# One projection of an attention layer by two levels of block products, with its operand sums formed on GpSimd

## The chip, the cores and the metric

The kernel runs on one core of a Trainium2 chip. The core's engines work side by side, each through its own queue in order: TensorE multiplies matrices and writes its sums to PSUM, VectorE and ScalarE move results out of PSUM and do elementwise work, GpSimd (POOL in the profile) does elementwise work on SBUF, and SyncE (SP) issues most of the DMA transfers between DRAM and SBUF. The metric is the device time of one execution in microseconds. Three runs of the kernel before took 1883.57 to 1885.51 us, with a median of 1883.69.

## The reference

Input x is 8 images of 512 channels and 32 x 32 = 1024 places, in float32. Four layers follow one another:

- Layer 0: a linear attention with 64 channels, scaled by the largest singular value, and a residual.
- Layer 1: group normalization, then attention over the 1024 places with 512 channels:

```python
h = _group_norm(x, gamma, beta).reshape(B, C, N)
q, k, v = wq h + bq, wk h + bk, wv h + bv
attn = softmax(q^T k * C ** -0.5)
out = x + wp (v attn^T) + bp
```

- Layer 2: attention with 128 channels, and a residual.
- Layer 3: signs of x times signs of a 512 x 512 matrix, scaled, and a leaky slope.

The kernel multiplies wq and wk once, into a 512 x 512 matrix wu. The scores of layer 1 are then h^T u with **u = wu h + bu**, a 512 x 512 by 512 x 1024 product for each of the 8 batches. This u is what the change is about.

## The kernel before

**Stages.** A setup computes statistics of layer 0 over all batches, wu and wo = wv wp, and their block sums. Then `fast` runs once for each batch, in the order 6, 7, 0, 1, ..., 5. It computes for one batch: the scores of layer 1 (`scores1`), v (`make_v`), the values and the residual (`values1`), the projections of layer 2 (`project2`), its scores (`scores2`), its values (`values2`), their projection back (`close2`, L683), and layer 3 (`leave`). Work of the next batch is woven in by generators that are stepped at fixed places: `entering` (the end of layer 0 and the normalization), `make_u` for its u, and the previous batch's last half of layer 3 (`rest3`).

**Block products.** `seven` multiplies two matrices, each cut into 2 x 2 blocks, with seven block products in place of eight. It needs sums of blocks: `sums_of` makes S1 to S4 of the left factor, `differences_of` makes T1 to T4 of the right one, on VectorE. The seven products are, in order, A11 B11, S1 T1, S2 T2, S4 B22, S3 T3, A12 B21, A22 T4. Each is accumulated in PSUM by `product_of` (matmuls at L396). `seven` moves results out on ScalarE (L348, L350) and adds them on VectorE (L354, L356). For u the left blocks are 256 x 256 blocks of wu (kept with su, their sums, in SBUF), the right ones 256 x 512 blocks of h (h and hs). `make_u` does it in two passes of 128 output rows each: 2 x 7 block products of 2 matmuls on 512 columns, 28 matmuls for a batch. It has 14 steps. At the last, `sums_of` forms S1 to S4 of u itself (tile us), because u is the left factor of the next batch's scores. S1 is the sum of the two quarters u's second column half consists of (below: c12, upper channels, and c22, lower channels); c21, the lower quarter of the first half, is needed only for S4.

**Where the steps of u stand.** `fast` steps `make_u` once at each of the last three steps of `project2`, once after every second tile of `scores2` (four times), once ahead of the values, once after them, twice inside `leave`, and the rest after `close2` of the second half. So steps 1 to 8 lie among the projections and scores of layer 2, and steps 9 to 14 at the batch's end, right before the next batch's `scores1`, which needs the whole u.

**What sets the order.** In the main part a scheduler orders each engine's queue, by priority in the order of the program text and by its own idea of when inputs are ready; waits on semaphores are put in by it. At run time every queue is in order. PSUM has eight banks of 128 x 512; an access to one half of a bank is ordered after earlier accesses to the other half.

**GpSimd before.** It has 109 instructions: the setup's constants, small powers (L236, L1085, L1182), and the residual sums of `values1` (L578, L604) and, in the last batch, of `leave` (L743).

**SyncE before.** In the order of its queue for each batch: a store and two loads around the inverse row sums of each attention (`inverse_sums`, L847 to L855), the stores of the output (L761), the loads of the next x (L139) and of f (L292).

After all batches a branch (`verdict`) leads to a general version of the whole computation if a row sum is out of bounds.

Of the kernel before, what the change touches and what calls it, by code (L numbers as in the profile page):

```python
# [16 lines left out]
P = 128  # L17
B = 8
C = 512
N = 1024  # L20
CC = C // P
NT = N // P
HF = 512
# [62 lines left out]
def kernel(  # L86
# [17 lines left out]
    nc = tc.nc  # L104
    mm = nc.tensor.matmul
# [17 lines left out]
    def bank():  # L123
        return psum["bank"].tile([P, HF], F32, tag="bank", name="bank")
# [17 lines left out]
    def half(i):  # L142
        return bass.ts(i, HF)
# [100 lines left out]


    r_dram = [dram.tile([4, N // 4], F32, name=f"r_dram{i}") for i in range(2 * B)]
    f_dram = [dram.tile([P, HF], F32, name=f"f_dram{b}") for b in range(B)]
    gm = [keep.tile([P, P], F32, tag=f"gm{j}", name=f"gm{j}") for j in range(NPAIR)]
    gs_, gh_ = (
# [18 lines left out]

    wu = wpool.tile([P, CC, C], F32, tag="wu", name="wu")
# [5 lines left out]
    su = wpool.tile([P, 3, 2, C // 2], F32, tag="su", name="su")  # L277
    so = wpool.tile([P, 3, 2, C // 2], F32, tag="so", name="so")


# [195 lines left out]
    def split_h(env, ht):  # L476
        hs = env["big"].tile([P, 3, 2, HF], F32, tag="hs", name="hs")
        b = [ht[:, chunks[k], half(n)] for k in range(2) for n in range(2)]
        return differences_of(b, [hs[:, i] for i in range(3)])

    def make_u(env, hb, got):

        ut = env["big"].tile([P, CC, N], F32, tag="uv", name="ut")
        wa = weights["u"]

        def done():
            us = env["big"].tile([P, 3, 2, HF], F32, tag="us", name="us")
            got.append(
                sums_of(quarters_of(ut, chunks, [half(0), half(1)]), [us[:, i] for i in range(3)])
            )  # L490

        for i in range(2):
            term = product_of(
                lambda a, b, q, k: wa[a][:, k, bass.ts(i, P)],
                lambda a, b, q, k: hb[b][:, k, :],
            )
            yield from seven(
                term,
                ut[:, i, half(0)],
                ut[:, i, half(1)],  # L500
                ut[:, 2 + i, half(0)],
                ut[:, 2 + i, half(1)],
                bu[:, i : i + 1],
                bu[:, 2 + i : 3 + i],
                then=done if i else None,
            )

    def make_v(hb, vt):

# [383 lines left out]
    def fast(env, n, hb, ua):  # L893
# [43 lines left out]
        for k, _ in enumerate(values1(env, xt, vt, es, r, scratch)):  # L937
            chore(k in (2, 7, 9, 11, 13))
            if k == 5 and more:
                nxt = resident[order[n + 1]]  # L940
                hb = split_h(env, normal(env, nxt))
        signs = None
        if more:
            steps = make_u(env, hb, got)
        else:
            signs = unpacked(env)

# [642 lines left out]
    with ExitStack() as main:  # L1590
        psum_pools(main, 0, 8)
        big = main.enter_context(tc.tile_pool(name="big", bufs=1, reuse_waits="tile"))
        epool = main.enter_context(tc.tile_pool(name="epool", bufs=EBUFS))
        small = main.enter_context(tc.tile_pool(name="small", bufs=3))
        env.update({"big": big, "e": epool, "small": small})
        got = []
        hb = split_h(env, normal(env, resident[order[0]], True))

        for k, _ in enumerate(make_u(env, hb, got)):
            if k in (1, 4, 7, 10, 13):  # L1600
                next(behind)
        ua = got[0]
        for n in range(B):
            hb, ua = fast(env, n, hb, ua)

# [113 lines left out]
    with tc.If(verdict[0] > 0):  # L1719
        with (  # L1720
            ExitStack() as stack,
            tc.tile_pool(name="gbig", bufs=1) as big,
            tc.tile_pool(name="gepool", bufs=4) as epool,
            tc.tile_pool(name="gsmall", bufs=2) as small,
        ):
            env = {"big": big, "e": epool, "small": small}
            psum_pools(stack, 2, 4)

            for a in (weights["u"], weights["o"]):
                nc.vector.tensor_tensor(a["S3"], a["A11"], a["S3"], ALU.subtract)  # L1730
            for b in range(B):
                xt = load_x(b)
                general(env, xt, b, channels(out[b]))
# [42 lines left out]
```

## Time and profile before

| | |
|---|---|
| median of three runs | 1883.69 us |
| profiled execution, its own time | 1883.24 us |
| its span, from first to last instruction | 1881.5 us |
| TensorE busy | 1857.0 us |
| VectorE busy | 1118.1 us |
| ScalarE busy | 545.7 us |
| GpSimd busy | 121.8 us |
| DMA traffic | 66.51 MB |
| granted TensorE clock, mean | 0.997 |

The page's first part gives for each engine its busy time, its share of the span and its number of instructions. A group's line names the source line, the engine, the operation, output and inputs, the form and the count, then the busy time and the mean length of one in ns, and the idle time of the engine ahead of the group with what ended it. A line of the timeline gives start, length, engine, source line and count, and in brackets the idle time ahead of it and its releaser. Consecutive matmuls overlap in the records, so one's cost is read from the distance of starts. In the timeline, one batch's u goes from 566 us to 637 us.

### The profile page before, as it was taken

How to read it: one execution, taken by the hardware profiler on the slowest of the kernel's cores; microseconds unless marked ns; L12 is line 12 of the kernel's file. 1: busy time of each engine (PE TensorE's matmuls, PEld its weight loads, DVE VectorE, ACT ScalarE, POOL GpSimd, SP SyncE). 2: the span in 40 equal slices, each digit the busy share in tenths (PEclk: the TensorE clock that was granted, in tenths of full speed). 3: DMA queues.
4: the chain of work that ended last, by engine and by line, in shares of the span. 5: the costliest groups of instructions: out<-in, count | busy, mean ns of one | idle time of the engine just before them, and what ended most of it. 6: DMA issues, size and time to landing. Idle time of an engine off the chain costs nothing.

```text
span 1881.5 us, 16558 instructions
## 1 busy us (share of the span) xinstructions
PE 1857.0 (99%) x6244; PEld 952.1 (51%) x6244; DVE 1118.1 (59%) x2077; ACT 545.7 (29%) x888; POOL 121.8 (6%) x109
## 2 busy tenths in 40 slices
PE   8998999999999999999999999999999999999997
PEld 3365455544645455544645455544645464544653
DVE  3256776467764676567764676357643666355447
ACT  2142221144202521244202522144202521244113
POOL 1000001100020000100020001100020001000011
PEclk9999999999999999999999999999999999999999
DMA  8420000002000200002000200001000200000001
GB/s 324 161 79 7 1 18 1 1 34 73 12 1 12 84 23 1 1 34 73 12 1 11 78 30 0 1 34 67 12 0 12 90 12 0 1 34 23 12 0 47
DMA packets 25203, 66.51 MB, mean 35 GB/s; under 512 B 3553, under 2 KB 4765, under 8 KB 24477
## 3 DMA queue, kind: packets, MB, share of 16 engines
q1 hardware_dynamic: 24188, 64.96, 9.5%
q8 instruction: 51, 0.84, 0.2%
q10 hardware_dynamic: 864, 0.43, 0.1%
q14 instruction: 36, 0.29, 0.0%
q0 software_dynamic: 64, 0.00, 0.0%
HBM read 46.44 MB, written 18.94 MB: 35 GB/s over the span
## 4 chain that ended last, share of the span: by engine, by line
PE 96%; DVE 2%; ACT 1%; issue 0%; DMA 0%; POOL 0%; DVEq 0%; ACTq 0%
PE bank L396 46%; PE bank L565 21%; PE bank L967 6%; PE bank L814 6%; PE bank L1354 5%; PE bank L666 3%; PE bank L683 3%; PE bank L420 1%; PE bank L706 1%; PE wide L1394 1%; PE bank L1450 1%; PE bank L1035 1%; PE bank L837 0%; PE quad L1248 0%; PE bank L1141 0%
## 5 line engine op out<-in xcount | busy, mean ns | idle before, releaser
L565 PE MATMUL bank<-e,vt 128*128 128x512 f32 x768 | 336.2, 594 | 0.0
L565 PEld LDWEIGHTS bank<-e,vt 128*128 128x128 f32 x768 | 144.3, 190 | 172.3 <-issue 167.9
L396 PE MATMUL bank<-ut,h 128*128 128x512 f32 x384 | 178.3, 597 | 0.0
L396 PEld LDWEIGHTS bank<-ut,h 128*128 128x128 f32 x384 | 71.3, 190 | 95.2 <-issue 93.5
L814 PE MATMUL bank<-tpg 128*128 128x512 f32 x256 | 115.4, 595 | 0.0
L396 PE MATMUL bank<-us,hs 128*128 128x512 f32 x256 | 115.3, 592 | 0.0
L967 PE MATMUL bank<-e,tpg 128*128 128x512 f32 x256 | 114.7, 595 | 0.0
L354 DVE TENSOR_TENSOR e<-bank,e 128x512 f32<-128x512 f32 x96 | 66.1, 689 | 63.2 <-PE bank L396 44.7
L821 ACT ACTIVATE e<-bank 128x512 f32<-128x512 f32 x128 | 76.3, 597 | 67.0 <-PE bank L814 67.0
L396 PE MATMUL bank<-wo,h 128*128 128x256 f32 x384 | 89.9, 384 | 0.0
L348 ACT COPY e<-bank 128x512 f32<-128x512 f32 x96 | 56.1, 584 | 115.0 <-PE bank L396 114.6
L396 PE MATMUL bank<-h,wu 128*128 128x512 f32 x192 | 89.4, 595 | 0.0
L236 POOL TENSOR_TENSOR r_r<-r_v,minus_half 128x4 f32<-128x4 f32 (+1 forms) x11 | 10.9, 988 | 1073.4 <-DVE r_v L235 1067.9
L967 PEld LDWEIGHTS bank<-e,tpg 128*128 128x128 f32 x256 | 48.1, 190 | 60.4 <-issue 60.0
L396 PEld LDWEIGHTS bank<-us,hs 128*128 128x128 f32 x256 | 48.6, 190 | 58.4 <-issue 55.7
L396 PEld LDWEIGHTS bank<-wo,h 128*128 128x128 f32 x384 | 71.4, 190 | 12.6 <-issue 3.8
L826 DVE TENSOR_TENSOR esum<-esum,e 128x1024 f32<-128x1024 f32 x48 | 58.8, 1225 | 30.2 <-ACT e L821 30.0
L814 PEld LDWEIGHTS bank<-tpg 128*128 128x128 f32 x256 | 47.6, 190 | 55.0 <-issue 52.4
L694 ACT ACTIVATE sg<-xt,rb 128x512 f16<-128x512 f32 x64 | 44.2, 716 | 107.4 <-DVE xt L685 104.5
L354 DVE TENSOR_TENSOR vt<-bank,vt 128x512 f32<-128x512 f32 x48 | 33.2, 691 | 67.3 <-PE bank L396 66.6
L348 ACT COPY vt<-bank 128x512 f32<-128x512 f32 x64 | 37.3, 583 | 122.3 <-PE bank L396 122.3
L348 ACT COPY ut<-bank 128x512 f32<-128x512 f32 x48 | 28.1, 585 | 123.4 <-PE bank L396 123.4
(367 smaller groups left out, 2927.0 us busy)
## 6 DMA issues: line engine op xcount, KB each, us to landing
xt<-in_x SPq DMA_DIRECT2D x55, 512.0 KB
out<-both SPq DMA_DIRECT2D x63, 256.0 KB
rfull<-r_dram SPq DMA_DIRECT2D x15, 512.0 KB
f_dram<-f SPq DMA_DIRECT2D x8, 256.0 KB
fb<-f_dram SPq DMA_DIRECT2D x8, 256.0 KB
w<-in_w SPq DMA_DIRECT2D x1, 1024.0 KB
q<-in_w_q SPq DMA_DIRECT2D x1, 1024.0 KB
k<-in_w_k SPq DMA_DIRECT2D x1, 1024.0 KB
```

What stands on the lines that cost most here:

```text
L348: nc.scalar.copy(dst, ps)
L354: nc.vector.tensor_tensor(dst, ps, u, ALU.add)
L396: mm(out=ps[:, q * w : (q + 1) * w], lhsT=lt(ka, kb, q, k), rhs=rhs(ka, kb, q, k), start=first and q == 0 and k == 0, stop=last and k == 1 ...
L565: mm(out=ps, lhsT=a[:, t, bass.ts(r_, P)], rhs=e[t], start=first and t == 0, stop=last and t == NTH - 1, skip_group_check=True,)
L666: mm(out=ps[:, i, :], lhsT=xt[:, cc, bass.ts(4 * h + i, P)], rhs=sbw["tpg"][:, cc, 2 * P : 3 * P], start=cc == 0, stop=cc == CC - 1,)
L683: mm(out=ps, lhsT=sbw["z"][:, bass.ts(oc, P)], rhs=att, start=True, stop=True)
L694: nc.scalar.activation(sg[:, cc, :], xt[:, cc, half(h)], AF.Sign, bias=rb3[:, cc : cc + 1])
L814: mm(out=ps, lhsT=pt[:, 0, bass.ts(t, P)], rhs=tt[:, 0, half(h)], start=True, stop=True,)
L821: nc.scalar.activation(e[:, half(h)], ps, AF.Exp, scale=float(P) ** -0.5)
L826: nc.vector.tensor_tensor(esum, esum, e, ALU.add)
L967: mm(out=banks[h], lhsT=gt[:, t, :], rhs=es[t][:, half(h)], start=t == 0, stop=t == NT - 1,)
L1354: mm(out=banks[i][side(h), :], lhsT=w0[i][:, cc, :], rhs=xt[:, cc, half(h)], start=cc == 0, stop=cc == CC - 1,)
```

## The change

For the first batch of the order u is made as before. For the other seven, `make_u2` takes the place of `make_u`:

- **Two levels.** Each of the seven block products (256 x 256 by 256 x 512) is itself done by seven products of 128 x 128 by 128 x 256 blocks (`inner`): 49 matmuls on 256 columns for a batch. `inner` uses two banks, p1 and p2, each for two half-bank results, in two steps: four products (A11 B11, S2 T2 in p1; S1 T1, S3 T3 in p2), then three (A12 B21 onto the first; S4 B22 and A22 T4 onto p2's). Three ScalarE copies and five VectorE sums of 256 columns follow each `inner`. In what follows, product i (0 to 6) is the i-th of the outer seven in the order of `pairs`.
- **Factors from DRAM.** The seven 128 x 128 factors of each outer block are made once, in the first batch's `scores1` (`factors_of_u`: four GpSimd sums and three stores for each of the seven), and stored in `fac_dram`. Each product's factors (448 KB) are loaded from there in each batch, into one of two buffers.
- **Sums of h on GpSimd.** `prepare_u` forms the inner T1 to T4 of a product's right block with three GpSimd instructions (128 x 512, 128 x 256, 128 x 256), into one of two buffers. The first two products are prepared in `values1` ahead of u, product i + 2 after product i's second step.
- **Sums of u on GpSimd.** The outer products 0, 1, 3 and 4 are written straight into quarters of u, the others into temporary tiles; the outer sums are then made in place by GpSimd instructions of 128 x 1024 (four for a batch) and 128 x 512 (five), and one VectorE instruction for the second half of product 6. c12 gets two of the 1024-wide sums after product 4, c22 one after product 5.
- **Storage.** wu and su move to a pool (`first_u`) that is closed after the first u; the buffers for factors and sums take its place. wu is stored to DRAM in the setup and loaded again in the general version only.

The number of steps stays 14, and so do the places where they are stepped.

```diff
+    wu_dram = dram.tile([P, CC, C], F32, name="wu_dram")
+    fac_dram = [dram.tile([P, 7, P], F32, name=f"fac_dram{i}") for i in range(7)]
...
+    def factors_of_u(env):
+        tt = nc.gpsimd.tensor_tensor
+        for i, (a, _) in enumerate(pairs):
...
+            tt(s[:, 0], a21, a22, ALU.add)
+            tt(s[:, 1], s[:, 0], a11, ALU.subtract)
+            tt(s[:, 2], a11, a21, ALU.subtract)
+            tt(s[:, 3], a12, s[:, 1], ALU.subtract)
+            nc.sync.dma_start(out=fac_dram[i][:, 0:2], in_=w[:, :, 0:P])
+            nc.sync.dma_start(out=fac_dram[i][:, 2], in_=a22)
+            nc.sync.dma_start(out=fac_dram[i][:, 3:7], in_=s)
+            yield
+
+    def prepare_u(env, hb, i):
+        jit = env["jit"]
+        fac = jit.tile([P, 7, P], F32, tag="fac", name="fac", bufs=2)
+        nc.sync.dma_start(out=fac, in_=fac_dram[i])
+        b = hb[pairs[i][1]]
+        t = jit.tile([P, 4, QF], F32, tag="jit", name="jit", bufs=2)
+        lo, hi = slice(0, QF), slice(QF, HF)
+        tt = nc.gpsimd.tensor_tensor
+        tt(t[:, 0:2], b[:, :, hi], b[:, 0, :].rearrange("p (i n) -> p i n", i=2), ALU.subtract)
+        tt(t[:, 2], b[:, 1, hi], t[:, 0], ALU.subtract)
+        tt(t[:, 3], b[:, 1, lo], t[:, 2], ALU.subtract)
...
+    def inner(made, d, bias=None):
...
+        pa = product(p1[:, lo], 0, True, False)
+        nc.scalar.copy(d21, pa)
+        pb = product(p1[:, hi], 2, False, True)
+        nc.vector.tensor_tensor(d21, pb, d21, ALU.add)
+        pc = product(p2[:, lo], 3, True, False)
+        nc.scalar.copy(d12, pc)
+        pd = product(p2[:, hi], 5, False, False)
+        plus(d22, pd, d21, 1)
+        nc.vector.tensor_tensor(d22, d22, d12, ALU.add)
+        yield
+        product(pa, 1, False, True)
+        ...
+        product(pc, 4, False, True)
+        plus(d12, pc, d21, 0)
+        product(pd, 6, False, True)
+        plus(d21, pd, d21, 1)
+        yield
+
+    def make_u2(env, hb, got, made):
...
+        for i, (a, _) in enumerate(pairs):
+            direct = {0: (1, 0), 1: (0, 0), 3: (1, 1), 4: (0, 1)}.get(i)
...
+            for j, _ in enumerate(inner(made[i], d, bias)):
+                if j:
+                    if i == 1:
+                        add(c11, c21)
+                    elif i == 4:
+                        add(c12, c21)
+                        add(c12, c22)
+                    elif i in (2, 5, 6):
+                        for k in range(2):
+                            tt = (nc.vector if i == 6 and k else nc.gpsimd).tensor_tensor
+                            tt(c21[:, k, :], c21[:, k, :], d[k], ALU.add)
+                        if i == 5:
+                            add(c22, c21)
+                    if i + 2 < 7:
+                        made.append(prepare_u(env, hb, i + 2))
+                    if i == 6:
+                        us = env["big"].tile([P, 3, 2, HF], F32, tag="us", name="us")
+                        got.append(sums_of(...))
+                yield
...
+            if n == 0 and k in (9, 11, 13, 15, 17, 19, 21):
+                next(late_u)
...
                 hb = split_h(env, normal(env, nxt))
+                if "jit" not in env:
+                    first_u.close()
+                    env["jit"] = main.enter_context(
+                        tc.tile_pool(name="jit", bufs=1, side="right", reuse_waits="tile")
+                    )
+                made_u = [prepare_u(env, hb, i) for i in range(2)]
...
-            steps = make_u(env, hb, got)
+            steps = make_u2(env, hb, got, made_u)
...
+        nc.sync.dma_start(out=wu_dram, in_=wu)
```

More of the change, by code (lines that the diff above doesn't have):

```diff
@@ L267 @@
     bb2 = const.tile([P, CC], F32, tag="bb2", name="bb2")
-    wu = wpool.tile([P, CC, C], F32, tag="wu", name="wu")
+    first_u = ExitStack()
+    upool = first_u.enter_context(
+        tc.tile_pool(name="first_u", bufs=1, side="right", reuse_waits="tile")
+    )
+    wu = upool.tile([P, CC, C], F32, tag="wu", name="wu")
     wo = wpool.tile([P, CC, C], F32, tag="wo", name="wo")
@@ L275 @@
     bvo = const.tile([P, CC], F32, tag="bvo", name="bvo")
-    su = wpool.tile([P, 3, 2, C // 2], F32, tag="su", name="su")
+    su = upool.tile([P, 3, 2, C // 2], F32, tag="su", name="su")
     so = wpool.tile([P, 3, 2, C // 2], F32, tag="so", name="so")
@@ L506, in make_u @@
             )
+    pairs = [
+        ("A11", "B11"),
+        ("A12", "B21"),
+        ("S2", "T2"),
+        ("S1", "T1"),
+        ("S4", "B22"),
+        ("S3", "T3"),
+        ("A22", "T4"),
+    ]
+    blocks = {"A11": 0, "A12": 1, "A22": 2, "S1": 3, "S2": 4, "S3": 5, "S4": 6}
+    QF = HF // 2
+    def factors_of_u(env):
+        tt = nc.gpsimd.tensor_tensor
+        for i, (a, _) in enumerate(pairs):
+            w = weights["u"][a]
+            a11, a12, a21, a22 = (w[:, k, bass.ts(m, P)] for m in range(2) for k in range(2))
+            s = env["small"].tile([P, 4, P], F32, tag="half_a", name="factors")
+            tt(s[:, 0], a21, a22, ALU.add)
[6 more added lines that the diff above has]
+            yield
@@ new lines, in prepare_u @@
+    def prepare_u(env, hb, i):
[9 more added lines that the diff above has]
+        tt(t[:, 3], b[:, 1, lo], t[:, 2], ALU.subtract)
+        rhs = {
+            "B11": b[:, 0, lo],
+            "B21": b[:, 1, lo],
+            "B22": b[:, 1, hi],
+            "T1": t[:, 0],
+            "T3": t[:, 1],
+            "T2": t[:, 2],
+            "T4": t[:, 3],
+        }
+        return fac, rhs
@@ new lines, in inner, with product, plus @@
+    def inner(made, d, bias=None):
+        fac, rhs = made
+        p1, p2 = bank(), bank()
+        lo, hi = slice(0, QF), slice(QF, HF)
+        (d11, d12), (d21, d22) = ((d[i][:, lo], d[i][:, hi]) for i in range(2))
+        def product(out, k, first, last):
+            a, b = pairs[k]
+            mm(
+                out=out,
+                lhsT=fac[:, blocks[a], :],
+                rhs=rhs[b],
+                start=first,
+                stop=last,
+                skip_group_check=True,
+            )
+            return out
+        def plus(dst, ps, x, i):
+            if bias is None:
+                nc.vector.tensor_tensor(dst, ps, x, ALU.add)
+            else:
+                nc.vector.scalar_tensor_tensor(dst, ps, bias[i], x, ALU.add, ALU.add)
+        pa = product(p1[:, lo], 0, True, False)
[9 more added lines that the diff above has]
+        product(pa, 1, False, True)
+        if bias is None:
+            nc.scalar.copy(d11, pa)
+        else:
+            nc.scalar.activation(d11, pa, AF.Identity, bias=bias[0])
+        product(pc, 4, False, True)
[3 more added lines that the diff above has]
+        yield
@@ new lines, in make_u2, with quarter, rows, add @@
+    def make_u2(env, hb, got, made):
+        ut = env["big"].tile([P, CC, N], F32, tag="uv", name="ut")
+        top, bottom = ([bu[:, 2 * k + i : 2 * k + i + 1] for i in range(2)] for k in range(2))
+        def quarter(k, h):
+            return ut[:, chunks[k], half(h)]
+        def rows(k, h):
+            return [ut[:, 2 * k + i, half(h)] for i in range(2)]
+        def add(dst, x):
+            nc.gpsimd.tensor_tensor(dst, dst, x, ALU.add)
+        c11, c12, c21, c22 = (quarter(k, h) for k in range(2) for h in range(2))
+        for i, (a, _) in enumerate(pairs):
+            direct = {0: (1, 0), 1: (0, 0), 3: (1, 1), 4: (0, 1)}.get(i)
+            if direct is None:
+                d = [
+                    env["small"].tile([P, HF], F32, tag="half_b", name="r") for _ in range(2)
+                ]
+            else:
+                d = rows(*direct)
+            bias = {1: top, 4: top, 5: bottom}.get(i)
+            for j, _ in enumerate(inner(made[i], d, bias)):
[15 more added lines that the diff above has]
+                        us = env["big"].tile([P, 3, 2, HF], F32, tag="us", name="us")
+                        got.append(
+                            sums_of(
+                                quarters_of(ut, chunks, [half(0), half(1)]),
+                                [us[:, k] for k in range(3)],
+                            )
+                        )
+                yield
@@ L941, in fast @@
                 hb = split_h(env, normal(env, nxt))
+                if "jit" not in env:
+                    first_u.close()
+                    env["jit"] = main.enter_context(
+                        tc.tile_pool(name="jit", bufs=1, side="right", reuse_waits="tile")
+                    )
+                made_u = [prepare_u(env, hb, i) for i in range(2)]
         signs = None
         if more:
-            steps = make_u(env, hb, got)
+            steps = make_u2(env, hb, got, made_u)
         else:
@@ L1602 @@
         ua = got[0]
+        late_u = factors_of_u(env)
         for n in range(B):
@@ L1727 @@
             psum_pools(stack, 2, 4)
-            for a in (weights["u"], weights["o"]):
-                nc.vector.tensor_tensor(a["S3"], a["A11"], a["S3"], ALU.subtract)
+            wu = big.tile([P, CC, C], F32, tag="wu", name="wu_again")
+            nc.sync.dma_start(out=wu, in_=wu_dram)
+            a = weights["o"]
+            nc.vector.tensor_tensor(a["S3"], a["A11"], a["S3"], ALU.subtract)
             for b in range(B):
```

## The prediction

> **What bounds the kernel now.** I read the page from the top: span and busy times, the chain that ended last, the groups of u, the timeline of one batch's end on TensorE, its busy times by stretch, and GpSimd's timeline.
>
> ```profile
> span 1881.5 us, 16558 instructions
> ...
> PE 1857.0 (99%) x6244; PEld 952.1 (51%) x6244; DVE 1118.1 (59%) x2077; ACT 545.7 (29%) x888; POOL 121.8 (6%) x109
> ...
> PE 96%; DVE 2%; ACT 1%; issue 0%; DMA 0%; POOL 0%; DVEq 0%; ACTq 0%
> ```
>
> TensorE holds 96% of the chain: work taken from it is gained in full, and each wait put on it is lost in full.
>
> ```profile
> L396 PE MATMUL bank<-h,wu 128*128 128x512 f32 x192 | 89.4, 595 | 0.0
> ...
> L396 PE MATMUL bank<-wo,h 128*128 128x256 f32 x384 | 89.9, 384 | 0.0
> ...
> L826 DVE TENSOR_TENSOR esum<-esum,e 128x1024 f32<-128x1024 f32 x48 | 58.8, 1225 | 30.2 <-ACT e L821 30.0
> ...
> L348 ACT COPY ut<-bank 128x512 f32<-128x512 f32 x48 | 28.1, 585 | 123.4 <-PE bank L396 123.4
> ```
>
> The mean (595, 384 ns) is one record's length; records overlap, so the cost is the distance of starts. A 1024-wide VectorE sum takes 1.22 us, a 512-wide ScalarE copy 0.585. The code issues 28 matmuls per batch for u, the four groups of u (192, 64, 128 and 64 records) make 448 = 8 x 56: an f32 matmul shows as two records.
>
> ```profile
> 630.68 3.60 PE L396 MATMUL bank<-h,wu 128*128 128x512 f32 x8
> ...
> 634.11 1.02 PE L396 MATMUL bank<-ut,h 128*128 128x512 f32 x2
> ...
> 1326.00 3.62 PE L396 MATMUL bank<-so,hs 128*128 128x256 f32 x16
> ...
> 1329.45 1.89 PE L396 MATMUL bank<-so,h 128*128 128x256 f32 x8
> ```
>
> (634.11 - 630.68) / 8 = 0.429 us a record at 512 columns, so 0.858 a matmul; (1329.45 - 1326.00) / 16 = 0.216 at 256, 0.432 a matmul.
>
> ```profile
> 558.00:606.00 48.00, 48.00 (x176) 25.75 (x175) 22.16 (x49) 14.86 (x26) 0.00 (x0) 1.00 0.00 0
> ...
> 620.40:644.50 24.10, 24.10 (x66) 10.59 (x65) 19.56 (x28) 15.33 (x24) 0.00 (x0) 1.00 0.11 44
> ```
>
> Columns: length, then busy PE, PEld, DVE, ACT, POOL. The first row is the stretch with u's first half, the second its end, up to the scores of the next batch. TensorE has no gap in either, but in the second VectorE is busy for 19.56 of 24.10: it has 4.5 us to give.
>
> ```profile
> 521.38 2.12 POOL L604 TENSOR_TENSOR xt<-xt,o_b 128x512 f32<-128x512 f32 x1 [3.16 <-issue]
> ...
> 522.29 2.36 DVE L609 TENSOR_TENSOR e<-e,scratch 128x512 f32<-128x512 f32 x2
> ...
> 541.61 1.26 POOL L578 TENSOR_TENSOR xt<-xt,o_b 128x512 f32<-128x512 f32 x1 [2.24 <-DVE r L1095]
> ...
> 545.41 2.18 POOL L578 TENSOR_TENSOR xt<-xt,o_b 128x512 f32<-128x512 f32 x1 [2.54 <-DVE o_b L576]
> ...
> 608.39 0.33 SPq L851 DMA_DIRECT2D rfull<-r_dram  x1
> ...
> 612.13 0.69 DVE L976 TENSOR_TENSOR att<-bank,rfull 128x512 f32<-128x512 f32 x1 [5.42 <-DMA rfull<-r_dram]
> ```
>
> A 512-wide GpSimd add takes 1.26 us, and 2.1 to 2.2 where VectorE reads two operands from SBUF at the same time; two L609 then took 2.36, elsewhere 1.29. A load of 512 KB is waited for 3.7 us after its issue.
>
> **The change, part by part (per batch, seven batches).**
>
> *TensorE work.* Removed 28 x 0.858 = 24.0 us, added 49 x 0.432 = 21.2: **-2.9 us** (-2.2 with the dearest 256-wide stretch, 16 records in 3.56 us from 697.92).
>
> *GpSimd.* Seven times one 512-wide and two 256-wide sums, then block sums: four of 1024 and five of 512. From 1.26: a 256 lies between 0.63 and 1.26 (I take 0.7), a 1024 between 1.26 and 2.52 (I take 2.5, as the width doubles). 7 x 2.7 + 4 x 2.5 + 5 x 1.26 = 35 us, where GpSimd was idle. As a mean over 85 us that fits; what counts is where the sums stand.
>
> *VectorE, ScalarE.* Five 256-wide VectorE operations per product, 0.42 each (L323 to L328 on sp: 416 to 424 ns), 14.7 us, plus one 512-wide (0.69), for six of 0.74 (L356): +11 us. ScalarE: 21 copies of some 0.37 (between the 0.26 of 128 columns and 0.585 of 512) for eight of 0.6: +3 us. Products 4 to 6 put 7 us of VectorE work into the end stretch for 2.2: more than its 4.5 us of room.
>
> *Middle, products 0 to 3.* In the built program TensorE's queue holds first product, second, then other work, then the third, which waits for ScalarE's copy of the first (same bank): 0.43 + 0.17 until the result is there + 0.03 + 0.37 + 0.3 from a release to the next matmul (e at 647.59, ut,hs at 647.91) = 1.3 us. Between them stand 0.7 to 1.7 us of scores and projections, so 0 to 0.6 us is missing at each; I take 0.3 x 4 = **+1.2**.
>
> *The end, products 4 to 6.* In the built program TensorE's queue from product 4 to the scores' S3 group holds 21 products (9.1), 16 sign matmuls (0.216 each: 3.5), four L683 (3.4) and six score matmuls (5.1): 21.1 us of work, nothing else to fill in. Walked with the durations above, zero at product 4:
> - TensorE reaches product 4's last matmul at 8.0 (done 8.4). Its sum stands on VectorE behind two rounds (but for the last L757) of L718, L719, two L727, two L757 (0.42, 0.69, 1.4, 1.5: 4.0 us each), and ends at 12.0.
> - Product 5's fifth matmul waits for the VectorE sum behind that one (12.4 + 0.3): TensorE, free at 10.1, idles 2.6. Product 6's factors, whose buffer is freed at 8.6, come at 8.7 + 3.7 = 12.4, hidden behind this; if that cover were gone they would cost 2.
> - GpSimd's queue: c12 += c21 and c12 += c22 for product 4 (12.0 to 17.0), two adds of product 5 that wait for its last sum (VectorE, 18.7), c22 += c21: 17.0 to 22.5. Only then can VectorE form S1 (1.22), to 23.7, and its successors are queued behind it: the sums of product 6 that the last product waits for, S2 and S3.
> - TensorE has nothing left at 20.4 and gets S1 at 24.0. Two S1 and two S2 matmuls (3.4), product 6's last (0.4), four sign matmuls (0.9) and 0.2 of waiting for a copy bring it to the S3 group at 29.0.
>
> 29.0 - 21.1 = 7.9 us. One VectorE operation with two SBUF operands (L757) meeting c12 += c21 adds 1.2. I take **+8.5**. Lower bound from GpSimd alone: after product 4's last matmul 0.6 + 2.4 + 2.4 + 2.5 + 2.4 + 1.6 (S1 and hand-overs) = 12 us against 8.2 of TensorE work, so 3.8. Upper: each of four such meetings costs a whole GpSimd sum's 1.2, and VectorE enters the scores late: 13.
>
> The Trainium skill, "SBUF — State Buffer", section "SBUF: two separate sides", says that the port pair shared by the two engines is locked for a whole instruction. By it a meeting costs up to the 2.5 of the new sums, three of them 7.5, and the sum would be near 1980. "TensorE: Matmul & The Clock Gate", Part 1, has the clock halve after an idle window of about 3.4 us; with one such window a batch, an estimate from that page is 1.7 us more each, 12 in all, about 1942. The row here does not show it: the granted clock reads 1.00 from 0 to 5 us too, although TensorE is idle for 4.89 of them.
>
> *Queues.* On SP each batch has seven more loads (448 KB; 1.8 us at the 256 GB/s of 650 to 655); the next batch's first two wait for products 5 and 6 ahead of the last stores and the x loads; those end by 660 (DMA share 0.80 from 655, 0.00 from 660) and L420 begins at 661.74, 2 us of room, while the two loads (3.6 us) start some 10 us ahead: nothing, at most 2. Ahead of the row sums' small store stands product 5's load, long released: 0 to 1 us, taken as nothing. On GpSimd two preparations (5.4 us) stand before the xt adds of L604 (516.96), whose xt is read at 545.25 (L336): nothing. Once: 28 GpSimd sums of 128 columns (0.3 to 1.26 each: 9 to 35 us) and 22 stores (4.2 MB, 16 us), under the first batch's scores, where GpSimd and the DMA are idle. The branch at the end isn't taken.
>
> **Sum.** 7 x (-2.9 + 1.2 + 8.5) = +47.6 on the profiled execution's 1883.24 (span 1881.5; the median of the runs is 0.45 above): **1930**.
>
> **Rivals.**
> - *GpSimd keeps up* (the other side): its sums finish behind other work, TensorE waits only as in the middle. 1883 - 20 + 8 = 1871. It decides once all waits of a batch are under 2.9 us. For it: GpSimd is 6% busy. Against: the chain of five sums has a floor of 9.7 us, with 8.2 of cover.
> - *Only the last factor load is late*: 2 us a batch, 1883 - 20 + 14 + 8 = 1885. For it: that load can't start before product 4 ends. Against: VectorE is late as well, at the same place.
> - *VectorE becomes the bound of the end*: locks and queue make it 13 us a batch, 1883 + 7 x 11.3 = 1962. For it: 19.56 of 24.10 before. Against: its tight operations read one operand from PSUM, which no row shows slowed.
> - *Mild*: only the GpSimd floor counts, 3.8 and 0.4 in the middle: 1883 + 7 x 1.3 = 1892.
>
> **How the numbers follow.** Forecast (1905 to 1950) 0.58; VectorE bound (over 1950) 0.17; mild (1888 to 1905) 0.16; GpSimd keeps up 0.06; late load 0.03, mostly within 0.2%. Two runs of this kernel differ by 0.1%, so 0.2% (3.8 us) is about what can be told from no change. Faster 0.06, within 0.03, slower 0.91. The range 1894 to 1970 leaves out the last two, part of the mild one and the far end of the VectorE case.
>
> **What would show it.** After: TensorE's waits at the first matmuls on us for VectorE, 3 to 5 us seven times; VectorE's S1 waiting for GpSimd's sum of ut; u's 49 products of 256 columns at 0.216 a record; TensorE's busy sum 20 us lower and its share near 95%. Wrong if GpSimd's 1024-wide sums take well under 2.4 us, if the waits stand in the middle, or if TensorE has no gaps at a batch's end.

## The result and the profile after

The changed kernel takes 1984.05 us (median of four runs, 1983.30 to 1985.13) against 1883.63 for the kernel before: a ratio of 1.0532, 95% interval 1.0518 to 1.0545. It is slower, as forecast, but by 100 us and not by 47, and outside the range given (1894 to 1970).

The page of the changed kernel, span, busy times, and the chain that ended last:

```profile
span 1983.3 us, 17988 instructions
...
PE 1890.5 (95%) x6538; PEld 1018.9 (51%) x6538; DVE 1286.8 (65%) x2287; ACT 563.1 (28%) x979; POOL 448.0 (23%) x347
...
PE 80%; DVE 15%; DMA 1%; issue 1%; ACT 1%; POOL 1%; DVEq 0%; ACTq 0%; POOLq 0%; SPq 0%
```

TensorE carried 96% of the chain before and carries 80% now; VectorE went from 2% to 15%, GpSimd to 1% only. TensorE's busy time has *risen* by 33 us although its work fell. In part this is the clock: a matmul record that starts at a low clock lasts longer (at 512 columns 1.02 us on average in place of 0.60). So that sum is not a measure of work.

In the code of the changed kernel the matmuls of `inner` stand at L574, those of `seven` at L402 (before L396), the residual of layer 2 at L835 and L837 (before L683, L685), the signs and the end of layer 3 at L846 to L909 (before L694 to L757), the row sums of layer 2 at L978 (before L826), `inner`'s VectorE sums at L586 to L598, `prepare_u` at L551 to L553, the outer sums at L623 and L645, S1 to S4 at L329 to L334.

What TensorE's weight loads waited for, in its queue (total us, times, longest):

```profile
PEld bank L574 <- DVE r L593: 30.4, 9, 4.2
...
PEld bank L402 <- DVE us L329: 24.5, 7, 3.7
```

The first two are the two waits that the prediction walked to: product 5's fifth matmul waits for VectorE's sum, and the first matmul on us for S1. The mean lengths tell what happened to VectorE. Groups of the changed kernel:

```profile
L978 DVE TENSOR_TENSOR esum<-esum,e 128x1024 f32<-128x1024 f32 x48 | 76.4, 1592 | 6.9 <-ACT e L973 5.0
L623 POOL TENSOR_TENSOR ut<-ut 128x1024 f32<-128x1024 f32 x28 | 75.0, 2680 | 8.7 <-ACT both L902 7.6
...
L909 DVE SCALAR_TENSOR_TENSOR both<-up,ps,both 128x512 f32<-128x512 f32 x57 | 62.2, 1117 | 3.0 <-ACT both L902 3.0
...
L598 DVE TENSOR_TENSOR r<-r 128x256 f32<-128x256 f32 x21 | 24.4, 1161 | 0.2
L870 DVE TENSOR_SCALAR both<-both 128x512 f32<-128x512 f32 x28 | 23.6, 844 | 2.8 <-ACT both L869 2.8
```

Two of these groups in the kernel before:

```profile
L757 DVE SCALAR_TENSOR_TENSOR both<-up,ps,both 128x512 f32<-128x512 f32 x57 | 41.8, 753 | 13.2 <-ACT both L750 13.1
...
L718 DVE TENSOR_SCALAR both<-both 128x512 f32<-128x512 f32 x28 | 11.8, 421 | 18.3 <-ACT both L717 18.3
```

L978 took 1225 ns before, L909 753, L870 421. The first three VectorE groups read two operands from SBUF, but L870 reads only one: six of its 28 instructions met a 1024-wide GpSimd sum and took 2.39 us each. The groups that read an operand from PSUM kept their length (L593 on r: 408 ns on average). The end of one batch shows it in order; zero of the prediction's walk, product 4's first matmul, is 1317.51:

```profile
1317.51 0.59 PE L574 MATMUL bank<-h,fac 128*128 128x256 f32 x2
...
1325.60 2.46 DVE L909 SCALAR_TENSOR_TENSOR both<-up,ps,both 128x512 f32<-128x512 f32 x2
...
1326.09 1.42 POOL L551 TENSOR_TENSOR jit<-hs 128x512 f32<-128x512 f32 x1 [20.46 <-PE bank L574]
...
1330.88 5.11 POOL L623 TENSOR_TENSOR ut<-ut 128x1024 f32<-128x1024 f32 x2 [1.09 <-ACT both L902]
...
1331.12 1.22 PE L574 MATMUL bank<-h,fac 128*128 128x256 f32 x2 [3.39 <-DVE r L593]
...
1331.59 2.19 DVE L909 SCALAR_TENSOR_TENSOR both<-up,ps,both 128x512 f32<-128x512 f32 x1
...
1340.98 2.44 POOL L623 TENSOR_TENSOR ut<-ut 128x1024 f32<-128x1024 f32 x1
1341.14 2.57 DVE L598 TENSOR_TENSOR r<-r 128x256 f32<-128x256 f32 x1
1343.62 1.21 DVE L329 TENSOR_TENSOR us<-ut 128x1024 f32<-128x1024 f32 x1
...
1344.89 2.08 PE L402 MATMUL bank<-us,hs 128*128 128x512 f32 x2 [3.25 <-DVE us L329]
...
1347.62 4.05 PE L402 MATMUL bank<-us,hs 128*128 128x512 f32 x6
```

L598 takes 2.57 us where it needs 0.42: it starts after c22 += c21 on GpSimd and ends just after it (1343.71 against 1343.42). Likewise each L909 that meets a GpSimd sum. The reader also sees what follows the two waits: the six records from 1347.62 stand in a stretch that runs to 1351.50, 0.65 us apart where 0.43 is normal. The clock in this stretch (columns: length, busy times of PE, PEld, DVE, ACT, POOL, then the granted clock, DMA share, GB/s):

```profile
1317.50:1331.00 13.50, 10.23 (x39) 6.19 (x37) 11.77 (x19) 8.99 (x15) 3.66 (x4) 0.95 0.25 74
1331.00:1338.00 7.00, 6.88 (x15) 4.39 (x16) 7.00 (x10) 2.80 (x6) 4.91 (x3) 0.60 0.19 75
1338.00:1344.80 6.80, 3.07 (x12) 1.55 (x10) 5.01 (x7) 2.43 (x5) 4.98 (x3) 0.90 0.20 67
1344.80:1352.00 7.20, 7.11 (x13) 3.30 (x14) 5.64 (x9) 0.88 (x2) 2.08 (x1) 0.62 0.22 65
```

After each of the two waits of over 3 us in this batch the clock is near half for a while (0.60, 0.62); its mean over the whole run is 0.981, before it was 0.997.

**Where the 100 us lie.** I took for each TensorE record its distance to the next beyond the usual one of its form, and summed it by stretch. Over the seven batches that is 30.1 us in the middle (products 0 to 3: 8.3, 6.4, 4.9, 4.7, 2.0, 2.0, 1.8) and 91.8 at the end (product 4 to the S3 group: 12.6 to 13.8 each). 30.1 + 91.8 - 20 of saved work = 102, against 100.4 measured.

### The profile page after: what moved, and what is told of

The parts are those of the page before. It is cut to its first block, busy times and chain, and to the rows that moved or that the text cites. A ratio compares the mean times of both kernels' runs of the same rounds, so it can differ in the third digit from the quotient of the medians.

```text
span 1983.3 us, 17988 instructions
## 1 busy us (share of the span) xinstructions
PE 1890.5 (95%) x6538; PEld 1018.9 (51%) x6538; DVE 1286.8 (65%) x2287; ACT 563.1 (28%) x979; POOL 448.0 (23%) x347
## 4 chain that ended last, share of the span: by engine, by line
PE 80%; DVE 15%; DMA 1%; issue 1%; ACT 1%; POOL 1%; DVEq 0%; ACTq 0%; POOLq 0%; SPq 0%
PE bank L402 35%; PE bank L717 19%; PE bank L1514 4%; PE bank L1127 4%; PE bank L574 4%; PE bank L818 3%; DVE esum L978 3%; PE bank L966 2%; DVE both L909 2%; PE bank L835 2%; PE bank L426 1%; DVE both L879 1%; DVE r L598 1%; DVE both L870 1%; PE wide L1554 1%
## 5 line engine op out<-in xcount | busy, mean ns | idle before, releaser
L402 PE MATMUL bank<-ut,h 128*128 128x512 f32 x384 | 183.2, 609 | 0.0
L402 PE MATMUL bank<-us,hs 128*128 128x512 f32 x256 | 131.8, 646 | 21.7 <-DVE us L329 21.7
L236 POOL TENSOR_TENSOR r_r<-r_v,minus_half 128x4 f32<-128x4 f32 (+1 forms) x11 | 10.9, 990 | 586.5 <-DVE r_v L235 493.8
L574 PE MATMUL bank<-jit,fac 128*128 128x256 f32 x392 | 121.2, 410 | 10.4 <-ACT r L595 2.8
L966 PE MATMUL bank<-tpg 128*128 128x512 f32 x256 | 120.0, 598 | 0.0
L402 PEld LDWEIGHTS bank<-ut,h 128*128 128x128 f32 x384 | 72.5, 194 | 88.8 <-issue 85.1
L1127 PE MATMUL bank<-e,tpg 128*128 128x512 f32 x256 | 116.5, 596 | 0.0
L574 PEld LDWEIGHTS bank<-jit,fac 128*128 128x128 f32 x392 | 73.9, 200 | 64.4 <-issue 36.0
L551 POOL TENSOR_TENSOR jit<-hs 128x512 f32<-128x512 f32 x21 | 27.9, 1330 | 325.2 <-PE bank L574 325.2
L402 PEld LDWEIGHTS bank<-us,hs 128*128 128x128 f32 x256 | 52.4, 209 | 84.0 <-issue 51.4
L402 PE MATMUL bank<-wo,h 128*128 128x256 f32 x384 | 89.9, 384 | 0.0
L846 ACT ACTIVATE sg<-xt,rb 128x512 f16<-128x512 f32 x64 | 45.8, 720 | 125.3 <-DVE xt L837 122.4
L978 DVE TENSOR_TENSOR esum<-esum,e 128x1024 f32<-128x1024 f32 x48 | 76.4, 1592 | 6.9 <-ACT e L973 5.0
L402 PEld LDWEIGHTS bank<-wo,h 128*128 128x128 f32 x384 | 71.4, 190 | 12.6 <-issue 3.8
L623 POOL TENSOR_TENSOR ut<-ut 128x1024 f32<-128x1024 f32 x28 | 75.0, 2680 | 8.7 <-ACT both L902 7.6
L1127 PEld LDWEIGHTS bank<-e,tpg 128*128 128x128 f32 x256 | 47.8, 190 | 53.0 <-issue 52.2
```

Of the source, the lines that this page charges most:

```text
L402: mm(out=ps[:, q * w : (q + 1) * w], lhsT=lt(ka, kb, q, k), rhs=rhs(ka, kb, q, k), start=first and q == 0 and k == 0, stop=last and k == 1 ...
L574: mm(out=out, lhsT=fac[:, blocks[a], :], rhs=rhs[b], start=first, stop=last, skip_group_check=True,)
L623: nc.gpsimd.tensor_tensor(dst, dst, x, ALU.add)
L966: mm(out=ps, lhsT=pt[:, 0, bass.ts(t, P)], rhs=tt[:, 0, half(h)], start=True, stop=True,)
L978: nc.vector.tensor_tensor(esum, esum, e, ALU.add)
L1127: mm(out=banks[h], lhsT=gt[:, t, :], rhs=es[t][:, half(h)], start=t == 0, stop=t == NT - 1,)
```

## The experiments

The theories. **G**: GpSimd's chain of sums at the end has too little work beside it. **L**: VectorE operations with two SBUF operands and GpSimd's sums hold each other up. **V**: VectorE's queue, in order, is the bound of the end, with L's blocked time in it. **C**: the half clock after the waits is on the path. A third pair of buffers, so that factors and sums could be prepared earlier, has no result: it needs 22.5 KB of a partition, where 15.9 were left. The kernel before took 1883.04 to 1885.32 us beside these runs. Each experiment's time is that of one execution; the four of the changed kernel differ by 1.8 us, those of the kernel before by 2.2.

**1. Without the outer sums.**

```diff
-                    if i == 1:
-                        add(c11, c21)
-                    elif i == 4:
-                        add(c12, c21)
...
-                            add(c22, c21)
                     if i + 2 < 7:
```

All outer sums are left out, GpSimd's and VectorE's, so u is incomplete, and the branch to the general version is kept from being taken.

> The outer sums of u (nine GpSimd instructions and one VectorE instruction a batch) are left out, so u lacks terms; the branch to the general version is held shut. If GpSimd's sums set the end of a batch (theory G), the wait for S1 goes and with it 7 to 9 us a batch; the wait of product 5's fifth matmul stays: about 1984 - 7 x 8 = 1928. If VectorE's own queue sets it (theory V), the same sums of 256 columns stand in it and it gains 2 or 3 a batch: above 1960. If the last factor load sets it (theory D), nothing changes: 1980.

Measured: 1915.04 us, below even what G expected. The outer sums, with all that follows from them, cost 69 us, 9.9 a batch; the wait for S1 is gone. Since their chain and their meetings with VectorE went together, this run doesn't tell G from L. But 32 us over the kernel before remain, and so does the other wait:

```profile
PEld bank L574 <- DVE r L593: 29.3, 7, 4.2
```

That wait therefore isn't due to the outer sums. In this run VectorE's queue in front of that sum still holds L909 and L879, held up by the three sums of `prepare_u`.

**2. Outer sums of products 4 to 6 on VectorE.**

```diff
-                        add(c12, c21)
-                        add(c12, c22)
+                        nc.vector.tensor_tensor(c12, c12, c21, ALU.add)
+                        nc.vector.tensor_tensor(c12, c12, c22, ALU.add)
...
-                            tt = (nc.vector if i == 6 and k else nc.gpsimd).tensor_tensor
+                            tt = (nc.vector if i > 2 else nc.gpsimd).tensor_tensor
```

(c22 += c21 likewise.)

> The outer sums of products 4, 5 and 6 move from GpSimd to VectorE (1.22 us for 1024 columns in place of 2.7, 0.69 for 512 in place of 1.3 to 1.5). Theory G: the chain before S1 is shorter by about 3 x 1.4 + 2 x 0.6 = 5.4 us a batch: about 1946. Theory V: VectorE's queue gets 5.5 us more of work a batch, which it has not got: 1984 or more.

Measured: 1968.59, between the two. GpSimd's chain at the end is gone altogether, and yet only 2.2 us a batch come back: a 1024-wide sum takes 1.22 us in place of 2.4, but now stands in VectorE's queue. The wait for S1 is 16.1 us in total (24.5), that for L593 31.4 (30.4). GpSimd's speed alone is not the cause.

**3. Steps twice as early.**

```diff
         def between(t):
-            fill(t % 2)
+            fill()
```

> One step of u after each tile of the second scores in place of one after each second tile: products 4 and 5 then lie among the second layer's scores and values, and only product 6 stands at the batch's end. Theory G: the chain of GpSimd sums is covered by other matmuls, the loss at the end falls from 13 to about 3 a batch, while the middle loses some 2 to 4 more as GpSimd gets less time per product: about 1984 - 7 x 7 = 1935. Theory V: VectorE is busier among the scores, the loss moves there: 1970 or more.

Measured: 1969.92, at V's edge. S1 is early now and nobody waits for it; instead TensorE waits at the end for `sg`, the signs of the residual. Timeline of this kernel:

```profile
1333.30 1.21 DVE L333 TENSOR_TENSOR ut<-ut 128x1024 f32<-128x1024 f32 x1
...
1335.69 0.68 DVE L837 TENSOR_TENSOR xt<-bank,xt 128x512 f32<-128x512 f32 x1
...
1337.18 0.59 PE L858 MATMUL bank<-sg,sw 128*128 128x512 f16 x1 [5.94 <-ACT sg L846]
```

VectorE is without a pause, and the residual sum L837 stands behind layer 3 and S3. With u's matmuls moved away, TensorE has nothing to do meanwhile: they were the cover of VectorE's work there.

**4. TensorE kept busy in both waits.** Eight matmuls whose results nobody reads:

```diff
+        def keep_warm(n, of):
+            ps = bank()
+            for _ in range(n):
+                mm(out=ps, lhsT=wo[:, 0, 0:P], rhs=of, start=True, stop=True)
...
+                if i == 6 and j:
+                    keep_warm(4, last)
                 yield
+                if i == 5 and not j:
+                    keep_warm(4, wo[:, 0, :])
```

(`last` is product 5's second half.)

> Adds eight matmuls without use (four of 256-column and 512-column f32 moving data each, results never read) in the two places of a batch's end where TensorE waits, so that it is not idle there; all else as in the changed kernel. Theory C (the half clock that follows each wait of over 3 us is on the path): of the two windows per batch, the one ahead of S1 falls into another wait, the one or two behind S1 (3.4 to 6.8 us at half speed) cost 1.7 to 3.4 us each batch: 1984 - 7 x (1.7 to 3.4) = 1960 to 1972, with the mean clock near 0.99. Rival (the half clock is hidden by the next wait): 1982 to 1990, although the mean clock rises as well.

Measured: 1997.69, a miss for both. The second group ran later than meant, moved other matmuls and overran the wait, so it says nothing on C there. The first group says something clear: with TensorE at full clock through the first wait, S1 starts at 1351.77, 26.12 us after product 4's first matmul (1325.65), as in the changed kernel (1343.62 - 1317.51 = 26.11):

```profile
1325.65 0.59 PE L574 MATMUL bank<-h,fac 128*128 128x256 f32 x2
...
1351.77 1.21 DVE L329 TENSOR_TENSOR us<-ut 128x1024 f32<-128x1024 f32 x1
```

In the other batches, too, S1 is no earlier than in the changed kernel (26.0 to 27.0 against 25.9 to 26.1). The half clock after the first wait is off the path; VectorE sets S1's time.

**5. All steps of u before the values of layer 2.**

```diff
-            fill(k > 5)
+            fill(k > 1)
...
-            fill(t % 2)
+            fill()
```

> All 14 steps of u are stepped before the values of layer 2 (one after each tile of the projections and scores), so that products 4 to 6 no longer stand at the batch's end. Theory G (what costs is that GpSimd's chain of sums has nothing beside it at the end): the end's 12 to 13 us per batch go, some 2 of the saved 2.9 come through, 1890 to 1905. Theory V (VectorE's queue is late wherever the sums stand, as its other work is ordered among them): half of the loss at most is got back, 1935 to 1970.

Measured: 1983.45, far from G and above V's range: nothing is won. The loss in products 0 to 3 falls to 0.5 us a batch, the rest grows to 15 to 20: products 4 to 6 now wait among the scores (2.0, 1.7 and 1.0 us in one batch). These waits are for `inner`'s own results on VectorE and ScalarE (L588, L595, L586); the first and the third stand on VectorE behind an L598 of 2.2 and 2.3 us that meets a GpSimd sum. And the end waits 6.6 us for `sg`.

**6. All sums on VectorE, and 7. that with the steps of experiment 5.**

```diff
-        tt = nc.gpsimd.tensor_tensor
+        tt = nc.vector.tensor_tensor
...
-                        add(c11, c21)
+                        nc.vector.tensor_tensor(c11, c11, c21, ALU.add)
```

(the same for all other outer sums.)

> All inner and outer sums of u on VectorE, places of the steps as in the changed kernel; GpSimd adds nothing for u any more. VectorE gets some 19 us more each batch, some 8 of it at the end, and its operations there meet no GpSimd sum (6.7 us less at the end). Theory L (meetings of the two engines are a main part of the loss): 1945 to 1962, and the 1024-wide sums L978 are back at 1.23 us. Theory V (VectorE's work itself is the bound of the end, 20.6 busy of 24.1 already): 1970 or more.

> Both edits: all steps of u before the values of layer 2, all sums on VectorE. In scores2 VectorE has some 26 us of room of 48; the whole u asks for some 40. Theory L: below the run with early steps alone by the cost of the meetings, 3 to 6 us a batch, and if the end is clean 1875 to 1895. Theory V: VectorE becomes the bound of scores2, 14 us a batch over, 1960 or more, above the run with early steps alone.

Measured: 1970.68, in time at the edge of V, but with the lengths that L had named, and 1957.38: 3.7 us a batch below experiment 5, as L had it, but the end isn't clean. Groups of the first of them:

```profile
L978 DVE TENSOR_TENSOR esum<-esum,e 128x1024 f32<-128x1024 f32 x48 | 58.5, 1220 | 6.3 <-ACT e L973 6.1
...
L909 DVE SCALAR_TENSOR_TENSOR both<-up,ps,both 128x512 f32<-128x512 f32 x57 | 41.4, 753 | 1.3 <-ACT both L902 0.9
...
L598 DVE TENSOR_TENSOR r<-r 128x256 f32<-128x256 f32 x21 | 8.7, 413 | 0.1
```

1592 is back at 1220, 1117 at 753, 1161 at 413: with no sum of u on GpSimd all their lengthening is gone, and L870's too (423), which shows L's mechanism. The sums that moved are 131 us of VectorE work by their groups, 19 a batch, yet all its groups together rise by only 33: in the changed kernel VectorE stood still for GpSimd for some 100 us. As it works in place of standing, only 13 us of time come back. And a new wait shows:

```profile
PEld bank L574 <- DMA fac<-fac_dram: 22.5, 7, 3.3
```

The last factor load, hidden behind VectorE until then, is late by 3.2 us a batch. In the second kernel the meetings are gone and products 0 to 3 lose 0.3 us; from product 4 on, which now stands among the scores, 14 to 19 us are lost in the first four batches and 10 in the last three, two thirds of these 10 in one wait:

```profile
1314.69 1.23 DVE L329 TENSOR_TENSOR us<-ut 128x1024 f32<-128x1024 f32 x1 [0.17 <-PE bank L1127]
...
1317.56 1.22 DVE L333 TENSOR_TENSOR ut<-ut 128x1024 f32<-128x1024 f32 x1
1318.70 1.22 DVE L334 TENSOR_TENSOR us<-ut,us 128x1024 f32<-128x1024 f32 x1
...
1324.35 0.68 DVE L837 TENSOR_TENSOR xt<-bank,xt 128x512 f32<-128x512 f32 x1
...
1328.64 1.81 PE L858 MATMUL bank<-sg,sw 128*128 128x512 f16 x3 [6.65 <-ACT sg L846]
```

u is complete long before, but S1 can't be formed before the values' last matmul (L1127): the tile us takes the place of tpg, which that matmul reads. So S1 to S4 fall between the residual's halves however early u is made.

**8. TensorE kept busy in the wait for S1 alone.**

```diff
+                if i == 0 and ka == "S1" and "idle" in env:
+                    of, extra = env.pop("idle"), bank()
+                    for _ in range(6):
+                        mm(out=extra[:, 0:QF], lhsT=wo[:, 0, 0:P], rhs=of, start=True, stop=True)
                 return term(ps, ka, kb, first, last)
```

> Six matmuls without use (256 columns, their data product 6's first result, written some 4 us before S1; 0.43 us each, 2.6 in all) stand right before the first matmul on S1, in the 3.25 us that TensorE waits there; the other matmuls keep the order of the changed kernel. In it, TensorE takes 7.5 us from S1's arrival for 4.7 us of work. Theory C (that is the half clock): 2 to 2.75 us per batch come back, 1965 to 1970. Rival (the stretch is slow because of waits for banks and sums, the clock costs nothing): 1982 to 1986.

Measured: 1973.23, 10.8 us faster than the changed kernel by doing more: C, at a smaller size than expected. In none of the seven batches is the clock at half after S1 any more. Here S1 to S3 in TensorE, with product 4's first matmul at 1310.45:

```profile
1338.61 3.60 PE L402 MATMUL bank<-us,hs 128*128 128x512 f32 x8
...
1343.78 1.95 PE L402 MATMUL bank<-us,h 128*128 128x512 f32 x4 [0.71 <-DVE us L334]
```

The eight records on S1 and S2 stand 0.43 us apart (1338.61 to the next work at 1342.05), and the S3 group comes at 33.3 instead of 35.8. From S3 on VectorE is late again (0.71), which takes a part back: 1.5 us a batch remain as gain.

**9. VectorE without L909.**

```diff
-                        nc.vector.scalar_tensor_tensor(
-                            yq, uq, ps3[:, oc : oc + 1], yq, ALU.mult, ALU.add
-                        )
+                        if signs is not None:
+                            nc.vector.scalar_tensor_tensor(
+                                yq, uq, ps3[:, oc : oc + 1], yq, ALU.mult, ALU.add
+                            )
```

> Leaves out the last operation of layer 3 on VectorE (the multiply-add of both and up, L909) in all batches but the last; all else as in the changed kernel. At a batch's end L909 holds VectorE for 5.9 us, 3.1 of it blocked by GpSimd's sums, ahead of the sums that products 5 and 6 wait for. Theory V (VectorE's in-order queue with the meetings in it sets the end): S1 comes 3 to 5 us earlier, 1984 - 7 x (3 to 5) = 1949 to 1963, and the wait of product 5 shrinks from 4.2 to some 1 us. Theory G (GpSimd's own chain sets it): product 4's last sum comes 2 us earlier at most, its chain takes the same time, 1970 to 1984.

Measured: 1940.54, 43.5 us less, more than V expected. No sum of u and no GpSimd instruction is touched. Product 4's first matmul and S1, and TensorE's weight queue, in this kernel:

```profile
1292.45 0.59 PE L574 MATMUL bank<-h,fac 128*128 128x256 f32 x2
...
1313.83 1.21 DVE L329 TENSOR_TENSOR us<-ut 128x1024 f32<-128x1024 f32 x1
```

```profile
PEld bank L574 <- DMA fac<-fac_dram: 13.0, 7, 1.9
...
PEld bank L402 <- DVE us L329: 6.5, 7, 1.9
...
PEld bank L574 <- DVE r L593: 2.6, 9, 0.5
```

The wait for L593 falls from 30.4 to 2.6, that for S1 from 24.5 to 6.5, and again the factor load comes to light; other waits grow (L595 to 13.6, S4's L334 to 10.9). S1 starts at 21.4 after product 4 (1313.83 - 1292.45), 4.7 earlier, and the S3 group at 29.3. What was ahead of u's sums in VectorE's queue set the end. L909 held VectorE there for 5.9 us, of which 3.0 are its own work, so this run alone doesn't tell its work from its lengthening by GpSimd; S1 comes earlier by more than the work. Part of the gain is clock as well: TensorE has no gap of more than 1.7 us in these batches, and the clock is at half in only four stretches, against fourteen in the changed kernel.

**10. The kernel before with GpSimd sums that nobody waits for.**

```diff
+    def idle_sums(env, xt, h):
+        spare = env["small"].tile([P, 2, 480], F16, tag="spare", name="spare", bufs=1)
+        for k in range(2):
+            x = xt[:, 2 * k : 2 * k + 2, half(h)][:, :, 0:480]
+            nc.gpsimd.tensor_tensor(spare, x, x, ALU.add)
...
             close2(xt, att, 0)
+            idle_sums(env, xt, 0)
...
             close2(xt, att, 1)
+            idle_sums(env, xt, 1)
```

> The kernel before, with four GpSimd sums of 128 x 960 per batch added that nobody waits for (two after the residual of each half of layer 2). It measures what meetings alone cost. Theory L (a meeting holds VectorE until GpSimd's sum ends, and VectorE has 4.5 us of room at the end): VectorE's two-operand operations there lengthen by 4 to 7 us a batch in all, 0 to 2.5 us of it reach TensorE, 1884 to 1902. Rival (meetings alone cost nothing, it is the new waits on the sums): 1882 to 1886 and the operations keep their length.

Measured: 1888.93, 5.3 over the kernel before and within L's range. In each batch just one VectorE operation met such a sum, S1 (1.21 us before):

```profile
1269.38 3.65 POOL L691 TENSOR_TENSOR spare<-xt 128x960 f16<-128x960 f32 x2 [13.47 <-DVE xt L685]
...
1271.67 2.44 DVE L323 TENSOR_TENSOR us<-ut 128x1024 f32<-128x1024 f32 x1
```

It starts 0.5 us into the second sum and ends 1.08 us after it: VectorE stood until that sum was over. One meeting of 1.2 us costs TensorE 0.73 us a batch (ahead of the scores' matmuls on ut and hs, seven times), although no instruction waits for the sums. No other VectorE group became longer by more than 0.5 us in total: the other operations missed the sums, which the expected 4 to 7 us had not foreseen.

## Why the prediction was wrong, step by step

- **Bound and direction: right.** TensorE bounds the kernel, a wait put on it is lost in full, and the two places named, product 5's fifth matmul and S1, are the two largest waits (S1 3.5 us on average, 3 to 5 named). S1 itself shows no wait for GpSimd's sum, as had been named: VectorE was held in L598 until that sum ended.
- **TensorE work, -2.9 a batch: right.** 49 matmuls as 98 records, 294 records more over seven batches for the 56 of each that went (6538 against 6244), and 0.43 to 0.44 us for two of them at full clock. The sign named for it, a busy sum 20 us lower, was wrong: it rose by 33, in part with the low clock.
- **GpSimd's durations: right alone, short in company.** A 1024-wide sum takes 2.34 to 2.44 us alone (2.5 taken), 2.68 on average, as GpSimd waits for VectorE too: a 512-wide sum of 1.27 alone took 2.08 beside S2 (L645 at 1345.34).
- **End, +8.5 a batch: the mechanism held, the size failed, measured 13.1.** (Its own terms, 7.9 and 1.2, add up to 9.1, of which it took 8.5.) Two terms failed. First one meeting, L757 with c12 += c21, at 1.2: up to S1 there are meetings worth 6.7 us (L909 2.8, L879 0.5, L598 1.2 and 2.2), since `prepare_u`'s three sums and c22's block VectorE as well, and a 256-wide operation pays the whole rest of a 1024-wide sum. So product 4's last sum ends at 13.2 (12.0 forecast), product 5's at 22.0 (18.7), S1's matmul starts at 27.4 (24.0). The row behind the 1.2 was a 512-wide sum's; a meeting is priced by the GpSimd instruction, here up to 2.2. Second, the clock, which the sum had at nothing: from S1 to the S3 group 8.4 us in place of 5.0, of which run 8 gives back 2.5 in the batch shown, and 1.5 a batch in time.
- **The Trainium skill, "SBUF — State Buffer", "SBUF: two separate sides"**, has the pair of ports locked for a whole instruction. The runs agree (2.57 for 0.42; run 10's 2.44 for 1.21). The estimate drawn from it, near 1980, was nearer than my sum, partly by luck: it stood for locks alone, and the runs share the loss out otherwise.
- **The Trainium skill, "TensorE: Matmul & The Clock Gate", Part 1**, has the clock halve after an idle window. The prediction set against it that the granted clock reads 1.00 in the idle first 5 us; that stretch, before TensorE's first work, was the wrong witness. The next two rows of the same view of the kernel before also read 1.00, and TensorE is busy in both throughout, but the first holds 17 records and the second 26:

```profile
5.00:10.00 5.00, 5.00 (x17) 2.66 (x19) 0.77 (x7) 1.28 (x1) 0.45 (x1) 1.00 1.00 348
10.00:15.00 5.00, 5.00 (x26) 2.66 (x24) 3.90 (x28) 0.58 (x1) 1.57 (x2) 1.00 1.02 416
```

  The records that start from 4.89 to 7.3 us last 0.92 to 1.12 us, those from 8.06 us on 0.59. This is the pace of half clock, so the 1.00 there is probably no reading of the clock. The rows after the two waits of the changed kernel read 0.60 and 0.62. The estimate of 12 us stands beside run 8's 10.8, partly by luck: it counted one stretch of 3.4 us a batch, and there were fourteen of 3.4 or 6.8 us, of which those after the first wait cost nothing.
- **Middle, +1.2 a batch: the last three batches lose 1.9, the first four 6.1.** In the first four VectorE also works on the singular values (transposes L1202, L1207), which the prediction's walk left out, and L978 meets GpSimd's sums. Timeline of such a stretch in the changed kernel:

```profile
844.31 4.17 DVE L978 TENSOR_TENSOR esum<-esum,e 128x1024 f32<-128x1024 f32 x2
...
845.15 2.25 POOL L645 TENSOR_TENSOR ut<-ut,r 128x512 f32<-128x512 f32 x1
```

  Two sums that take 2.4 alone hold VectorE for 4.2. That both together make up the 6.1 is read from the trace; a run without the singular values' work wasn't made. In experiments 5 and 7 this stretch loses 0.5 and 0.3. In experiment 6, with the steps in their old places and no sum of u on GpSimd, the first four batches still lose 6.3 on average, so meetings alone are not the cause; how the 6.1 divide stays open.
- **Factor load hidden, 2 us if its cover goes: right.** 3.2 and 1.9 in the two runs that took the cover away.
- **The other queues, nothing: right as far as the waits show.** Among TensorE's waits in the changed kernel a DMA's shows once, 4.6 us for a load of the setup. The load of the row sums does hold VectorE (att, L1136), and TensorE waits for that result 4.4 us in all, against 1.0 before.
- **The rivals.** What came is the rival "VectorE becomes the bound of the end", whose price of 13 us a batch at the end was met (13.1); 1962 was short of 1984 by the middle, 21.7 us more than allowed. Against it the prediction had held that VectorE's "tight operations read one operand from PSUM": true of most of them, but they stand in order behind L909 and behind L598, one of u's own sums, which read two from SBUF. "GpSimd keeps up" and "Mild" are out: in run 2 no outer sum of GpSimd stands in the chain, and 11 us a batch stay lost at the end.

Of the 54 us between forecast and result, 32 lie at the end (13.1 against 8.5, seven times) and 22 in the middle (30.1 against 8.4).

No version here beats the kernel before. The fastest that computes everything is run 7 with 1957; the 20 us of TensorE work saved are all there was to win, and the sums that they are bought with stand where VectorE had 4.5 us to give.

## What to carry to other kernels

Work moved to an idle GpSimd is not free for VectorE: count, at each place where the two run side by side, the VectorE operations with two SBUF operands, and those with one that show it (here a TENSOR_SCALAR, 2.39 us in place of 0.42), and price each at up to the whole GpSimd instruction, not at a share. Then walk the in-order queue of the engine that has the least room, with those prices in it, and see what stands ahead of the results that the bound engine waits for. A matmul scheme that saves a tenth of one stage in exchange for more results to be added pays only where the adding engine has room; and the matmuls of a stage are also cover for the work beside them, which lies bare once they are moved.

## What was unexpected of the hardware

- A wait of TensorE costs more than its length: after 3.25 us without work the following 7 us ran at a mean clock of 0.62, and six matmuls without use in that wait made the kernel 10.8 us faster.
- The low clock after the first wait cost nothing, as VectorE set the pace there: S1 came 26.1 us after product 4's first matmul with it and without it.
- A single long wait is not what decides on the clock here: after one wait of 3.33 us in the changed kernel (to 1109.77, in the fourth of the seven batches) it stayed at full, and in run 9 it fell to half four times in batches where no gap was longer than 1.7 us.
- A GpSimd sum that nobody waits for and that meets a single VectorE operation per batch made the kernel before 5.3 us slower.
